# A gated-experts layer on one core: the order of ScalarE's seedings in the first unit, the banks of its fourth slab, and the counts at which turnings and operand steps are issued

## The chip, the core and the metric

The kernel runs on one core of a Trainium2 chip. The metric is the device time of one execution in microseconds. Before the change it is 2478.14 us, the median of three runs (2477.49 to 2479.66). About 0.2% of that, 5 us, is what such a measurement can tell from no change.

## The reference, cut to what matters

There are eight sequences of 512 rows with 256 columns, eight experts and one shared expert, all in float32. Each expert multiplies by a gate matrix and an up matrix (256 x 1024), takes silu(gate) * up, and multiplies by a down matrix (1024 x 256). The experts' outputs are summed with a weight for each sequence and added to the input.

```python
E, B, S, D, F = (8, 2, 256, 256, 1024)   # the input that comes in is (8, 512, 256)
g = jnp.einsum('bsd,edf->ebsf', h, Wg)
u = jnp.einsum('bsd,edf->ebsf', h, Wu)
expert_outs = jnp.einsum('ebsf,efd->ebsd', jax.nn.silu(g) * u, Wd)
expert_output = jnp.einsum('be,ebsd->bsd', gating_probs, expert_outs)
shared = jnp.einsum('bsf,fd->bsd', jax.nn.silu(h @ Sg) * (h @ Su), Sd)
x = x + (1.0 - sg) * expert_output + sg * shared
```

## The kernel before, in words

**Units.** The work is cut into 36 units: two halves `h` of four sequences, nine experts `e` (the ninth is the shared one), two groups `g` of four 128-wide slabs of F. A unit computes silu(gate) * up for four slabs `i` and four sequences `j`, 16 combinations, and then their down products. Everything is held transposed, so a tile is 128 columns of F or D by 512 rows of a sequence.

**Fewer products by sharing.** With the 256 input columns in two halves, each combination would need two matmuls for gate (`m` = 0) and two for up (`m` = 1). The kernel saves some by a bilinear identity over pairs of slabs and sequences. The four "hub" combinations (i, i) take a product P (`P_step`, line 401) and a product Q into the same bank (`Q_step`, line 423). Each of the six pairs in `PAIRS` then takes three products for two combinations: R1 (`R1_step`, line 442), which goes into a bank that was *seeded* with a difference of two P's, and two products R (`R_step`, line 452). With the down products (three for each pair, lines 538, 522 and 561, and eight for the row and column sums, `p` and `q`) a unit has 78 matmuls. Float32 takes two passes, so the trace shows two records for each. In the steady stretch a unit takes 66.95 us (one unit's P at 1378.42, the next unit's at 1445.37), 0.86 us for each matmul.

**Who does what between.** ScalarE copies P to SBUF (line 406), takes silu (line 387, `finish` with m = 0), copies the finished hub bank D (line 429), seeds banks (`seed`, line 437) and copies or scales accumulators. VectorE forms the differences `f` of P's (lines 416 and 418; a slab's differences must be read before Q may go into that bank), multiplies silu by up (line 392, `finish` with m = 1, giving `h`), writes the second bank of a pair as D minus R1 (line 447) and adds D to the other one (line 457). GpSimd (POOL) forms the weights' differences and sums (`w_difference`, line 331; `w_sums`, lines 343 and 344, two of whose operands ScalarE scales at line 341 for three of the six pairs), the down weights' forms (`d_forms`), and the row and column sums of `h` (`add_sum`, line 479). In the first half's first unit it also forms `b` (line 251).

**Banks.** There are eight PSUM banks. Tags `g0` and `g1` have three each for gate and up; `po0` and `po1` are one each and take the down products and all transposes ("turnings"). `new_po` alternates between the last two; while a pair's first down product is `held`, everything else goes to the other one. Two engines' accesses to one bank are put in program order, two reads as well: where `Q_step` calls `finish` and then the copy of D, the copy waits for the multiply.

**The order.** A generator, `gate_up`, yields after each step of gate and up, and `down` after each down product. The strings `FIRST`, `ORDER` and `LAST` interleave them: G is one step of `gate_up`, D one step of `down` of the unit before or of this one. In a unit there are 16 hub steps (`HUB_STEPS`) with 8 D's among them, and then six blocks "GGDGGDGGD", one for each pair. In the first unit ("TGGTGGTGG", then 16 G's, then five blocks) the first D comes only after pair 0's block. `seed(u, 0)` is called ahead of P of slab 3, and `seed(u, p + 1)` at the head of block p. TensorE's and POOL's instructions keep the program's order throughout, ScalarE's in the first unit only; all the rest is ordered by the framework's planner, which works with its own cost estimates.

**The two counters.** `since_close` counts D's. From unit 2 on, at every fourth D one step of `prepare(1)` is taken, which makes the second half's operands: its 72 steps are, for each of four sequences, six (load, nothing, two turnings, nothing, store), and then for each of six pairs, eight (load, nothing, three with POOL subtracts and adds of 128 x 512, two with nothing, store). In the first unit of the second half (unit 18), where the count starts again at 0, the eight finished output blocks of the first half are turned back (`turn_back`, transposes at line 143 into a `po` bank, an add of the input at line 625, a store) at the D's in `BACK_AT`. There D 1 to 11 still belong to the unit before: p0, q0, three of pair 5, q1, p1, q2, p2, q3, p3. After that each pair of unit 18 takes three D's.

Of the kernel before, what the change touches and what calls it, by code (L numbers as in the profile page):

```python
# [9 lines left out]
F32 = mybir.dt.float32  # L10
# [6 lines left out]
def kernel(  # L17
# [37 lines left out]
    nc = tc.nc  # L55
# [322 lines left out]
        u.Ud[p] = U  # L378
        u.Wd[p] = {lo: W[:, 0], hi: W[:, 1]}

    def new_bank(u, m, name):
        return ps_g.tile([P, S], F32, tag=f"g{m}", name=f"{name}{m}_{u.name}")

    def finish(u, m, i, j, bank):
        if m == 0:
            s = spool.tile([P, S], F32, tag="sg", name=f"sg{i}{j}_{u.name}")
            nc.scalar.activation(s, bank, AF.Silu)  # L387
            u.sg[i, j] = s
        else:
            b = NI * u.h + j  # L390
            t = hpool.tile([P, S], F32, tag="h", name=f"h{i}{j}_{u.name}")
            ve.scalar_tensor_tensor(  # L392
                t, u.sg[i, j], coef[:, u.e, b : b + 1], bank, ALU.mult, ALU.mult
            )
            u.h_[i, j] = t


    def P_step(u, i, m):
        bank = new_bank(u, m, f"c{i}{i}")
        u.bank[i, i, m] = bank  # L400
        nc.tensor.matmul(  # L401
            bank, u.raw[i][:, m, 0], xhub[u.h, i][:, 0], start=True, stop=True
        )
        if i < 3:
            t = ppool.tile([P, S], F32, tag="p", name=f"P{i}{m}_{u.name}")
            nc.scalar.copy(t, bank)  # L406
            u.Ps[i, m] = t
        for p, (k, j) in enumerate(PAIRS):
            if max(k, j) == i:

                o = u.Ps[min(k, j), m]
                t = o
                if i < 3:
                    t = zpool.tile([P, S], F32, tag="z", name=f"f{k}{j}{m}_{u.name}")
                if k == i:
                    ve.tensor_sub(t, o, bank)  # L416
                else:
                    ve.tensor_sub(t, bank, o)
                u.f[p, m] = t

    def Q_step(u, i, m):
        bank = u.bank[i, i, m]
        nc.tensor.matmul(  # L423
            bank, u.at[i][:, m], xhub[u.h, i][:, 1],
            start=False, stop=True, skip_group_check=True,
        )
        finish(u, m, i, i, bank)
        t = ddpool.tile([P, S], F32, tag="dd", name=f"D{i}{m}_{u.name}")
        nc.scalar.copy(t, bank)  # L429
        u.Ds[i, m] = t  # L430

    def seed(u, p):

        i, j = PAIRS[p]
        for m in range(2):
            u.bank[j, i, m] = new_bank(u, m, f"c{j}{i}")
            nc.scalar.copy(u.bank[j, i, m], u.f[p, m])  # L437
# [23 lines left out]
    def h_sums(u, p):  # L461


        i, j = PAIRS[p]
        if not starred(u, p):
            return
        u.X[p] = tpool.tile([P, S], F32, tag="t", name=f"X{p}_{u.name}")
        ve.tensor_sub(u.X[p], u.h_[j, i], u.h_[i, j])  # L468
        for k, l in ((i, j), (j, i)):
            for which, n in (("rows", k), ("cols", l)):  # L470
                u.sums.append((which, n, (k, l)))
# [191 lines left out]
    def gate_up(u, nxt):  # L663

        def differences(p):
            x_difference(u, p)
            w_difference(u, p)

        def sums(p):
            x_sums(u, p)  # L670
            w_sums(u, p)

        for p, make in ((0, w_difference), (0, w_sums), (1, w_difference), (1, w_sums)):
            make(u, p)
        if u.n:
            make_at(u, 3)
        w_difference(u, 2)
        ahead = ((0, x_difference), (0, x_sums), (1, x_difference), (1, x_sums), (2, x_difference))
        if u.n:
            for p, make in ahead:  # L680
                make(u, p)
        step = 0
        for kind, i, m in HUB_STEPS:
            if kind == "P" and i == 3 and m == 0:
                seed(u, 0)
            if kind == "Q":
                Q_step(u, i, m)
            elif kind == "P":
                P_step(u, i, m)
                if u.n == 0 and m == 1 and i in (1, 3):  # L690
                    for p, make in ahead[:2] if i == 1 else ahead[2:]:
                        make(u, p)
            else:
                R1_step(u, 0, m)
            step += 1
            if step == 2 and u.n:
                make_ad(u)
            if step in (3, 5, 7, 9, 11, 13) and u.n:
                d_forms(u, (step - 3) // 2)
            yield  # L700
        if u.n == 0:
            make_ad(u)
            for p in range(len(PAIRS)):
                d_forms(u, p)
        for p in range(len(PAIRS)):
            last = p + 1 == len(PAIRS)
            if p + 3 < len(PAIRS):
                differences(p + 3)
            if nxt is not None:
                if p >= 2:  # L710
                    load_w(nxt, p - 2)
                    if p < 5:
                        make_at(nxt, p - 2)
            store_forms(u)
            if p == 5 and nxt is not None:
                load_d(nxt)
            if not last:
                seed(u, p + 1)
            for m in range(2):
                if not last:  # L720
                    R1_step(u, p + 1, m)
                elif nxt is not None:
                    P_step(nxt, 0, m)
                yield
                for r in range(2):
                    R_step(u, p, m, r)
                    if m == 1 and r == 1:
                        h_sums(u, p)
                        if p + 2 < len(PAIRS):
                            sums(p + 2)  # L730
                    yield
# [20 lines left out]

    ends = {}
    since_close = 1000
    BACK_AT = (4, 7, 10, 13, 15, 18, 21, 24)
    HAND = {mybir.EngineType.PE, mybir.EngineType.Pool}
    by_hand = ExitStack()
    by_hand.enter_context(
# [18 lines left out]
    for u in units:  # L777
        final = u.closes
        if u.opens and u.h:
            since_close = 0  # L780
        nxt = units[u.n + 1] if u.n + 1 < len(units) else None
        g = gate_up(u, nxt)
        nG = 0
        for what in FIRST if u.n == 0 else LAST if nxt is None else ORDER:
            if what == "G":
                if nG == TAKE:
                    for _ in behind:
                        pass
                    if u.opens:
                        acc = {}  # L790
                    behind = down(u, acc)
                if final and nxt is not None and nG in (18, 21, 24, 27):
                    load_x(u.h + 1, (nG - 18) // 3)
                if nxt is None and nG == 40:
                    for i in range(NI):
                        last_rows[i] = load_rows(
                            *((zpool, "z") if i < 3 else (iopool, "io")), NI * u.h + i
                        )
                if nG > TAKE and nG % 2 == 0 or nxt is None:
                    for _ in range(2 if nxt is None else 1):  # L800
                        if u.sums:
                            add_sum(u)
                if nG < TAKE and u.n and units[u.n - 1].sums:
                    add_sum(units[u.n - 1])
                next(g)
                nG += 1
            elif what == "T":
                for _ in range(2):
                    next(turning, None)
            elif what == "B":  # L810
                turn_back(u.h, *ENDS.pop(0))
            elif what == "X":
                i, j, pools = TAILS.pop(0)
                if pools:
                    tail_banks(j, pools)
                tail(u, i, j, bool(pools))
            elif what == "S":
                store_rows(STORES.pop(0))
            else:
                next(behind, None)  # L820
                since_close += 1
                if ahead is not None and u.n >= 2 and since_close % 4 == 0:
                    next(ahead, None)
                if u.opens and since_close in BACK_AT:
                    turn_back(u.h - 1, *BACK[BACK_AT.index(since_close)])
        for _ in g:
            pass
        if u.closes:
            for _ in ahead:
                pass  # L830
        if u.n == 0:
            by_hand.close()
            by_hand.enter_context(tc.manual_schedule(engines=HAND))
        for _ in turning:
            pass
# [37 lines left out]
```

## Time and profile before

| what | value |
|---|---|
| median of three runs | 2478.14 us |
| the profiled execution | 2474.26 us, its span 2472.4 us |
| granted TensorE clock, mean | 0.999 |
| PE busy | 2439.9 us, 99% |
| POOL busy | 2100.4 us, 85% |
| DVE busy | 1938.0 us, 78% |
| ACT busy | 1247.4 us, 50% |
| DMA | 103 GB/s mean; the main queue 33.7% of 16 engines' span |
| PE busy in 0 to 40 us / 40 to 80 us | 31.40 us / 36.06 us |
| PE busy in 200 to 1200 us | 995.86 us |
| PE busy in 1240 to 1280 us | 35.55 us |

TensorE is busy nearly all the time, so what can change is the little time in which it waits: at the start, where the two halves meet, at the end, and in single places between. Time at which another engine is idle costs nothing by itself. The last three rows are from the profile's table of stretches (its first rows end at 40, 60 and 80 us).

### The profile page before, as it was taken

The numbers are of one execution on the slowest core, as the hardware profiler recorded it, in microseconds if no ns is written. First come the engines' busy times: TensorE is split into PE (matmuls) and PEld (weight loads), VectorE is DVE, ScalarE is ACT, GpSimd is POOL, SyncE is SP. The second block draws the span as 40 slices with busy tenths as digits, with TensorE's granted clock in tenths as the row PEclk, the third lists the DMA queues.
The fourth block names the chain that finished last, engine by engine and source line by source line (L and its number), as shares of the span: only waits on it lengthen the run. The fifth ranks groups of instructions, "written<-read, shape, count | busy, mean of one in ns | idle before, by whom it ended". The sixth has DMA issues, their size and how long they took to land. (4 is left out here: it accounts for less than half of the span.)

```text
span 2472.4 us, 22803 instructions
## 1 busy us (share of the span) xinstructions
PE 2439.9 (99%) x5772; PEld 1082.1 (44%) x5772; DVE 1938.0 (78%) x2880; ACT 1247.4 (50%) x2305; POOL 2100.4 (85%) x2339
## 2 busy tenths in 40 slices
PE   8999999999999999999999999999999999999998
PEld 3444444444444444444444444444444444444444
DVE  6777777778777787877977777778777777777788
ACT  4554455455545555555445555555555555555552
POOL 7888888998899898888878888888888888888884
PEclk9999999999999999999999999999999999999999
DMA  4333334433333332333443333223333332233332
GB/s 155 93 97 96 111 117 125 132 124 109 112 111 116 99 113 86 102 98 113 126 132 94 94 90 94 85 90 99 102 102 103 94 102 90 85 94 90 94 95 76
DMA packets 180800, 255.81 MB, mean 103 GB/s; under 512 B 14016, under 2 KB 114368, under 8 KB 180672
## 3 DMA queue, kind: packets, MB, share of 16 engines
q1 hardware_dynamic: 180384, 254.33, 33.7%
q8 instruction: 48, 0.79, 0.1%
q14 instruction: 80, 0.66, 0.1%
q10 hardware_dynamic: 288, 0.04, 0.0%
HBM read 238.59 MB, written 15.73 MB: 103 GB/s over the span
## 5 line engine op out<-in xcount | busy, mean ns | idle before, releaser
L452 PE MATMUL c<-b,wb 128*128 128x512 f32 x1728 | 847.3, 592 | 0.8 <-DMA b<-xs 0.8
L387 ACT ACTIVATE sg<-c 128x512 f32<-128x512 f32 x576 | 343.8, 597 | 607.2 <-DVE c L457 346.0
L392 DVE SCALAR_TENSOR_TENSOR h<-sg,coef,c 128x512 f32<-128x512 f32 x576 | 428.1, 743 | 244.4 <-PE c L452 139.6
L452 PEld LDWEIGHTS c<-b,wb 128*128 128x128 f32 x1728 | 327.3, 190 | 409.4 <-issue 385.0
L442 PE MATMUL c<-v,u 128*128 128x512 f32 x864 | 442.5, 594 | 9.7 <-ACT c L437 9.7
L479 POOL TENSOR_TENSOR rows<-rows,h 128x512 f32<-128x512 f32 x284 | 374.7, 1319 | 0.0
L447 DVE TENSOR_TENSOR c<-D,c 128x512 f32<-128x512 f32 x432 | 299.2, 692 | 85.7 <-ACT sg L387 64.2
L479 POOL TENSOR_TENSOR cols<-cols,h 128x512 f32<-128x512 f32 x284 | 362.9, 1278 | 0.0
L457 DVE TENSOR_TENSOR c<-c,D 128x512 f32<-128x512 f32 x432 | 298.8, 692 | 20.1 <-PE c L452 19.9
L343 POOL TENSOR_TENSOR wb<-u,wb 128x256 f32<-128x256 f32 x108 | 80.2, 742 | 240.4 <-ACT wb L341 240.4
L401 PE MATMUL c<-x,w 128*128 128x512 f32 x576 | 276.5, 592 | 0.3 <-DVE x L166 0.3
L442 PEld LDWEIGHTS c<-v,u 128*128 128x128 f32 x864 | 163.2, 190 | 217.3 <-issue 171.1
L538 PE MATMUL r<-h,wd 128*128 128x512 f32 x428 | 218.7, 592 | 1.6 <-DVE accb L513 1.6
L468 DVE TENSOR_TENSOR X<-h,h 128x512 f32<-128x512 f32 x214 | 214.2, 1001 | 7.0
L561 PE MATMUL r<-X,ud 128*128 128x512 f32 x428 | 218.6, 592 | 0.0
L429 ACT COPY D<-c 128x512 f32<-128x512 f32 x288 | 168.3, 584 | 92.1 <-DVE h L392 92.1
L423 PE MATMUL c<-x,at 128*128 128x512 f32 x432 | 210.0, 595 | 0.9 <-DVE P L416 0.9
L479 POOL TENSOR_TENSOR rows<-h,h 128x512 f32<-128x512 f32 x144 | 197.5, 1371 | 0.0
L479 POOL TENSOR_TENSOR cols<-h,h 128x512 f32<-128x512 f32 x144 | 185.7, 1289 | 0.0
L406 ACT COPY P<-c 128x512 f32<-128x512 f32 x216 | 126.6, 587 | 104.7 <-PE c L401 100.4
L401 PEld LDWEIGHTS c<-x,w 128*128 128x128 f32 x576 | 109.1, 190 | 136.4 <-issue 112.4
L521 ACT COPY S<-accS 128x512 f32<-128x512 f32 x135 | 79.7, 590 | 155.4 <-DVE accV L509 145.6
(106 smaller groups left out, 3474.3 us busy)
## 6 DMA issues: line engine op xcount, KB each, us to landing
b<-xs SPq DMA_DIRECT2D x210, 512.0 KB, 3.6
v<-xs SPq DMA_DIRECT2D x210, 256.0 KB, 2.6
w<-in_L_cond_Wg_dram SPq DMA_DIRECT2D x128, 128.0 KB, 3.5
w<-in_L_cond_Wu_dram SPq DMA_DIRECT2D x128, 128.0 KB, 3.6
wd<-in_L_cond_Wd_dram SPq DMA_DIRECT2D x32, 512.0 KB, 4.9
xin<-in_x_dram SPq DMA_DIRECT2D x24, 256.0 KB, 3.7
f<-xd SPq DMA_DIRECT2D x24, 256.0 KB, 3.2
xs<-f SPq DMA_DIRECT2D x18, 256.0 KB, 2.1
```

The source lines that it names most:

```text
L387: nc.scalar.activation(s, bank, AF.Silu)
L392: ve.scalar_tensor_tensor(t, u.sg[i, j], coef[:, u.e, b : b + 1], bank, ALU.mult, ALU.mult)
L401: nc.tensor.matmul(bank, u.raw[i][:, m, 0], xhub[u.h, i][:, 0], start=True, stop=True)
L423: nc.tensor.matmul(bank, u.at[i][:, m], xhub[u.h, i][:, 1], start=False, stop=True, skip_group_check=True,)
L442: nc.tensor.matmul(bank, u.U[p][:, m], u.V[p], start=False, stop=True, skip_group_check=True)
L447: ve.tensor_sub(other, u.Ds[j, m], bank)
L452: nc.tensor.matmul(bank, u.W[p][:, r, m], u.VB[p][:, r], start=False, stop=True, skip_group_check=True,)
L457: ve.tensor_add(bank, bank, u.Ds[j, m])
L468: ve.tensor_sub(u.X[p], u.h_[j, i], u.h_[i, j])
L479: gp.tensor_tensor(sums[n], u.h_[n, n] if first else sums[n], u.h_[at], ALU.add)
L538: nc.tensor.matmul(po, w, b, start=True, stop=True)
L561: nc.tensor.matmul(A, u.Ud[p], u.X[p], start=False, stop=True, skip_group_check=True)
```

## The change

1. In the first unit the two P's of slab 3 go to the `po` banks, not the `g` banks.
2. In the first unit the seeds are issued earlier in ScalarE's order: pair 0's ahead of Q of slab 1, pair 1's ahead of P of slab 3, and pair p + 2's at the end of block p, ahead of the scalings of `w_sums(p + 2)`.
3. In the first unit, for m = 1, the copy of D comes ahead of `finish`, so the multiply on VectorE waits for the copy.
4. The turnings in unit 18 come at other D's.
5. A step of `prepare` comes at every fifth D.

```diff
-    def new_bank(u, m, name):
+    def new_bank(u, m, name, spare=False):
+
+        if spare and u.n == 0:
+            turned[m] = False
+            return ps_o.tile([P, S], F32, tag=f"po{m}", name=f"{name}{m}_{u.name}")
         return ps_g.tile([P, S], F32, tag=f"g{m}", name=f"{name}{m}_{u.name}")
...
-        bank = new_bank(u, m, f"c{i}{i}")
+        bank = new_bank(u, m, f"c{i}{i}", i == 3)
...
+        t = ddpool.tile([P, S], F32, tag="dd", name=f"D{i}{m}_{u.name}")
+        u.Ds[i, m] = t
+        if u.n == 0 and m == 1:
+            nc.scalar.copy(t, bank)
         finish(u, m, i, i, bank)
-        t = ddpool.tile([P, S], F32, tag="dd", name=f"D{i}{m}_{u.name}")
-        nc.scalar.copy(t, bank)
-        u.Ds[i, m] = t
+        if u.n or m == 0:
+            nc.scalar.copy(t, bank)
...
-            if kind == "P" and i == 3 and m == 0:
+            if (kind, i, m) == ("P", 3, 0) and u.n or (kind, i, m) == ("Q", 1, 0) and u.n == 0:
                 seed(u, 0)
+            if (kind, i, m) == ("P", 3, 0) and u.n == 0:
+                seed(u, 1)
...
-            if not last:
+            if not last and u.n:
                 seed(u, p + 1)
...
                         h_sums(u, p)
+                        if u.n == 0 and p + 2 < len(PAIRS):
+                            seed(u, p + 2)
                         if p + 2 < len(PAIRS):
                             sums(p + 2)
...
-    BACK_AT = (4, 7, 10, 13, 15, 18, 21, 24)
+    BACK_AT = (5, 7, 9, 11, 14, 17, 20, 23)
...
-                if ahead is not None and u.n >= 2 and since_close % 4 == 0:
+                if ahead is not None and u.n >= 2 and since_close % 5 == 0:
```

## The prediction

> **What bounds the kernel.** I read the engines' busy times first, then who PE waited for, then the first 80 us engine by engine, then each other place with a wait.
>
> ```profile
> PE 2439.9 (99%) x5772; PEld 1082.1 (44%) x5772; DVE 1938.0 (78%) x2880; ACT 1247.4 (50%) x2305; POOL 2100.4 (85%) x2339
> PE c L442 <- ACT c L437: 9.7, 6, 2.3
> PE q L538 <- POOL cols L479: 2.3, 1, 2.3
> PE pto L143 <- ACT accS L505: 1.9, 1, 1.9
> PE pto L143 <- DVE accB L509: 1.8, 2, 1.4
> PE pto L143 <- DVE accV L511: 1.6, 1, 1.6
> PE ptx L143 <- ACT accS L530: 1.0, 1, 1.0
> PE c L423 <- DVE P L416: 0.9, 2, 0.5
> ```
>
> PE is the bound, and the number of matmuls stays. So the ceiling is the waits, in all about 28 us (the list has some more at the two ends, which the change doesn't touch). The largest is R1 waiting for its seed, 9.7 us in six waits; PE's timeline has all six before 68 us: 2.31, 2.10, 1.35, 1.26, 1.26 and 1.38. The first shows the cause, and a second cost behind it:
>
> ```profile
> 24.61 0.59 ACT L429 COPY D<-c 128x512 f32<-128x512 f32 x1 [1.74 <-DVE h L392]
> 25.10 1.11 ACT L437 COPY c<-f 128x512 f32<-128x512 f32 x2
> 25.84 1.69 PE L442 MATMUL c<-v,u 128*128 128x512 f32 x2 [2.31 <-ACT c L437]
> 26.00:28.00 2.00, 2.00 (x3) 0.60 (x3) 2.00 (x4) 0.21 (x1) 1.92 (x5) 0.55 1.01 381
> 28.00:30.00 2.00, 2.00 (x4) 0.86 (x3) 1.52 (x3) 0.71 (x2) 1.84 (x4) 0.60 0.61 240
> 25.25 3.66 DVE L416 TENSOR_TENSOR P<-P,c 128x512 f32<-128x512 f32 x6
> ```
>
> The seed waits in ScalarE's fixed order behind the copy of D, which waits for VectorE's multiply. After the gap the granted clock (third column from the end in the two stretches) is halved for a while: R00, Q30 and R01 start at 25.84, 27.33, 29.04 and Q31 at 30.19, so 4.35 us for three products that take 2.57 at full clock, 1.8 us lost. The last line matters as much: the six differences that Q30 and Q31 wait for run only from 25.25 to 28.91.
>
> POOL is the second engine. It has no idle from 14.65 on but four waits, and 1.01 at 82.83:
>
> ```profile
> 38.83 1.27 POOL L251 TENSOR_TENSOR b<-v,x 128x512 f32<-128x512 f32 x1 [1.91 <-ACT sg L387]
> 47.26 1.27 POOL L251 TENSOR_TENSOR b<-v,x 128x512 f32<-128x512 f32 x1 [1.74 <-PE c L452]
> 56.48 1.27 POOL L251 TENSOR_TENSOR b<-v,x 128x512 f32<-128x512 f32 x1 [1.29 <-PE c L452]
> 65.70 1.27 POOL L251 TENSOR_TENSOR b<-v,x 128x512 f32<-128x512 f32 x1 [1.32 <-PE c L452]
> 100.28 1.27 POOL L479 TENSOR_TENSOR cols<-cols,h 128x512 f32<-128x512 f32 x1
> 103.12 1.02 PE L538 MATMUL q<-cols,ad 128*128 128x512 f32 x2
> ```
>
> The last pair is q2 of unit 1: its sum ends at 101.55, so POOL is only 1.5 us ahead of PE there.
>
> **The change part by part: the hub of the first unit.** PE ends P31 near 23.4 in both kernels. ScalarE is free at 18.85; pair 0's two copies (0.59 each, 0.49 apart) go from there to 20.0, silu 1 moves from 19.12 to 20.0, and the copies D11 and D21, no longer behind a multiply, end near 21.5 and 23. So no ScalarE work is late, R00 starts at 23.4 and not 25.84, and that 2.31 goes. What is late next is Q30. VectorE has no idle from 15.7 to 29.5, and the change takes no instruction from it; in whichever order the planner puts it (the multiplies now wait for the copies, so fillers will go first), the six differences end near 28.9 as before. So Q30 waits about 3 us from 24.2, Q31 starts at 28.95, and R1 of pair 1, whose seed is long there, at 29.85 and not 33.31: 3.5 us won of 2.31 + 2.10 + 1.8. Bounds: 1.7 us if the clock halves again in the new gap, 6.2 if the planner puts the 3.6 us of fillers (1.04, 1.75, 0.83) behind the differences. I take 3.5, since those fillers run first in the order of before.
>
> The clock row is where a rule and the trace differ. The Trainium skill's "TensorE: Matmul & The Clock Gate", "HAM oscillation", asks for no idle gaps of more than about 3.4 us; by that a gap of 2.3 costs no clock, and the sum would hold 2.31 + 2.10 only, with none of the 1.8 to win. This trace has the halved clock after 2.31 us of idle, and none after 2.10 us at 31.2. The same page ("Part 1") says that the windows run freely, which fits both. I go by the trace: the gap was dear, and the new one of 3 us may be; with the phase of before it falls over two windows (24.2 to 25.8 to 27.2), so I book no loss.
>
> P31 in a `po` bank costs nothing: the last turning's readers end at 17.6 and the first down product comes at 41.86, the bank is read out near 31. The multiply that now waits for the copy (0.59) adds no work: the order of two readers of a bank is turned round, and before the copy waited.
>
> **Blocks 0 to 4.** Block 0 runs from 29.85, six products, to 35.0. Pair 2's first seed follows silu of R001 (product ends 32.4, VectorE's add by 34.4 behind the two scalings' work of 1.6 us, silu to 35.0), so R1 of pair 2 starts at 35.6 against 40.04: 4.45 won. The second seed needs the bank of R011, its multiply ends near 38.5, the seed 39.1, just in time. From there each block drops its wait, 1.26 + 1.26 + 1.38 = 3.9, and I keep 0.35 for seeds that come a little late: 8.0 by PE's own chain. Queued behind the waiting second seed on ScalarE are the two scalings (0.72) and a silu; the scalings come at 39.8 where POOL wants them at 38.2, which makes it idle 1.3.
>
> **POOL's cap.** POOL's idle time until q2 of unit 1 is 1.91 + 1.74 + 1.29 + 1.32 + 1.01 = 7.27. All of it can go, less the 1.3 just named: 6.0. With the 1.5 of lead, PE can be 7.5 us earlier at q2, not 8.0. I take **-7.5** for the first unit; bounds -3.5 (hub alone, 1.7, and half the blocks) and -8.8 (7.27 + 1.5).
>
> **The turnings in unit 18.** Before, PE waits there 1.65 at D4 (the turning goes into the bank that D4 has just written, and two VectorE subtracts read it), 0.41 at D7, 0.47 at Q30 between, and 1.92 at D13 (again the second D of a pair). After, D14, 17, 20 and 23 are third D's, whose free bank was read out one or two products ago, and 9 and 11 have one that is long read. At D5 the turning's bank is free too, but its add (0.69) comes behind the close's three VectorE instructions (0.70 + 1.29), and q1 in that bank waits 0.7, Q30 0.1; D7 keeps 0.5. So 4.45 becomes 1.3: -3.1; bounds -4.4 and 0 (another 0.5 us at each of six turnings). The eight transposes and their DMAs stay the same in number; the first four loads of x land near 870 us, so the shorter spacing of 2 D's doesn't meet a load.
>
> **Steps of `prepare` at every fifth D.** The 72 steps end in unit 15 and not 13, before unit 17 needs them. A POOL step of 1.23 to 1.9 us placed after the last scaled weight of a unit (D20) and ahead of the next unit's D4 stands before q2's sum. Counting D's: before, three such (subtract, scale, two adds) fall before q2 of unit 10, and there PE waits the 2.28 at 713.60. Their time is 4.8 (starts of 679.66, 686.50 and 708.61 and the next ones), so the lead is 2.5. After, unit 12 and unit 15 have a subtract, a scale and one add each, 3.1 to 3.6: 0.6 to 1.1 each. Unit 9 has two adds: nothing. Sum 1.7 against 2.28. A turning right after the second D of a pair waits for a copy, 1.03 at 253.26 (unit 3, D13). After there are two, unit 2 D19 and unit 4 D22: 2.0. Loads on SP's queue move with the steps and can hold b back, as now 0.19 and 0.57: left equal. Together **+0.4**; bounds -2.5 and +3.
>
> **Sum.** -7.5 - 3.1 + 0.4 = -10.2 on the profiled execution's 2474.26: 2464.1. The median of the runs shown is 3.9 above that execution; carried over, 2468.0.
>
> **The rivals.** *The wait moves, not goes* (0.22): the hub's new Q30 gap halves the clock (1.7 left of 3.5), the seeds queue behind VectorE in each block, POOL's cap bites in unit 1, and turnings win half. -3.5 - 1.5 + 0.5 = -4.5: 2473.6. For it speaks VectorE's full row up to 29.5; against it that steady units run the same blocks with no wait. *More goes* (0.10): fillers later, POOL's full 8.8, turnings -4.4: about -13: 2465. *The plan tips* (0.08): VectorE's and ScalarE's order in 35 units is the planner's, and any edit ahead can shift it. The row that shows the price is Q30 waiting 0.47 for the differences, now in units 18 and 35 only; in the other 33 units that is 15.5 us, less the 10.2 won: +5.3, 2483.4. It decides from 0.31 us a unit on. Against it: the pattern repeats every unit with PE never idle. That the change does not do what it says in the first unit is excluded only as far as ScalarE's order there is by hand.
>
> **How the numbers follow.** The forecast has 0.60. About 0.2%, 5 us, is what the measurement can tell from no change. Faster: 0.60 + 0.10 + nearly half of 0.22 = 0.80; within: 0.12; slower: 0.08. Range: 2464 (case three, a little beyond) to 2474 (case two and the poorer ends of two terms); beyond lie the tipped plan and the tails.
>
> **What would show it.** Right: no row "c L442 <- ACT c L437" over 2 us in all, a new wait of 2 to 3 us of L423 on L416 before 30 us, PE reaching unit 1's first Q near 76 and not 83.4, POOL without its four waits, no 1.9 us in unit 18, waits of about 1 us at q2 of units 12 and 15 and after the turnings of units 2 and 4. Wrong: R1 still waiting for seeds, L423 waiting in every unit, or POOL more than 2 us behind at q2 of unit 1.

## The result, and the profile after

The changed kernel takes 2463.04 us, the median of five runs (2462.99 to 2464.21), against 2478.14 (2476.09 to 2479.66): a ratio of 0.9941, 95% interval 0.9927 to 0.9956. That is 15.1 us faster, 10.2 were forecast, and 2463.04 lies just under the range's lower end of 2464.

The profiled execution moved as forecast: 2464.21 us against 2474.26, so 10.05 less where the sum said 10.2. The 5 us that are missing in the forecast lie between profile and timed runs. The execution of after that was profiled is the slowest of its five runs. The one of before was 1.8 us faster than the fastest of its five.

The profile after, first the engines' busy times and then who PE waited for (total, times, longest). Line numbers have moved: R1 is now line 449, Q is 427, `seed` 444, `add_sum` 486.

```profile
PE 2439.2 (99%) x5772; PEld 1082.2 (44%) x5772; DVE 1936.5 (79%) x2880; ACT 1246.9 (51%) x2305; POOL 2100.1 (85%) x2339
PE q L545 <- POOL cols L486: 3.3, 4, 1.2
PE c L427 <- DVE P L420: 2.7, 3, 1.8
PE pto L143 <- DVE accB L516: 1.8, 2, 1.4
PE ptx L143 <- ACT accS L537: 1.8, 2, 0.9
PE c L449 <- ACT c L444: 0.7, 1, 0.7
```

The seeds' row, 9.7 us before, is down to 0.7 in one wait. The two turnings' rows of 1.9 and 1.6 are gone; that of `ptx` has grown from 1.0 to 1.8. Q's wait for VectorE has grown from 0.9 to 2.7, and q's for POOL from one wait to four.

The first unit, from the timelines of PE, VectorE, ScalarE and POOL in turn:

```profile
24.59 1.02 PE L449 MATMUL c<-v,u 128*128 128x512 f32 x2
27.39 1.12 PE L427 MATMUL c<-x,at 128*128 128x512 f32 x2 [1.78 <-DVE P L420]
25.47 3.67 DVE L420 TENSOR_TENSOR P<-P,c 128x512 f32<-128x512 f32 x6
46.85 0.59 ACT L444 COPY c<-f 128x512 f32<-128x512 f32 x1 [4.97 <-DVE h L396]
47.93 0.73 POOL L343 TENSOR_TENSOR wb<-u,wb 128x256 f32<-128x256 f32 x1 [0.64 <-ACT wb L341]
95.11 1.26 POOL L486 TENSOR_TENSOR cols<-cols,h 128x512 f32<-128x512 f32 x1
96.43 1.12 PE L545 MATMUL q<-cols,ad 128*128 128x512 f32 x2 [0.66 <-POOL cols L486]
```

R00 starts with no wait. Q30 then waits 1.78 us for the first half of the six differences, which VectorE runs from 25.47, 0.22 us from where it ran them before. One second seed of a block is issued late (46.85), after ScalarE has waited 4.97 us for VectorE's multiply on its bank, and costs PE 0.72. POOL has one idle of 0.64 left, and q2 of unit 1 waits for it: POOL's lead of 1.5 us is used up.

The clock was halved in this execution as well, but at the start. The line gives the stretch, the engines' busy times and, third from the end, the granted clock:

```profile
8.00:11.00 3.00, 3.00 (x4) 1.04 (x4) 0.00 (x0) 0.59 (x1) 1.25 (x5) 0.51 1.04 318
```

To place the gains, the table compares the start of each unit's first row-sum product, `p0`, between kernels. "Unit 1" is at 85.09 us in the first profile of before; a negative number is earlier.

| profile | unit 1 | unit 2 | unit 17 | unit 19 |
|---|---|---|---|---|
| after | -7.51 | -6.58 | -5.79 | -10.16 |
| after again (`e15_after_again`) | -8.48 | -7.63 | -6.91 | -11.30 |
| before again (`e1_before_again`) | +1.60 | +1.60 | +3.96 | +3.96 |
| before, third profile (`e11_before_look`) | -0.41 | -0.41 | +2.28 | +2.27 |
| before, fourth profile (`e12_before_look2`) | -0.55 | -0.55 | +2.04 | +2.03 |

After unit 19 every row stays as it is to the end.

### The profile page after: what moved, and what is told of

It is laid out like the page before. It is cut to its first block, busy times and chain, and to the rows that moved or that the text cites. A ratio compares the mean times of both kernels' runs of the same rounds, so it can differ in the third digit from the quotient of the medians.

```text
span 2462.3 us, 22810 instructions
## 1 busy us (share of the span) xinstructions
PE 2439.2 (99%) x5772; PEld 1082.2 (44%) x5772; DVE 1936.5 (79%) x2880; ACT 1246.9 (51%) x2305; POOL 2100.1 (85%) x2339
## 4 chain that ended last, share of the span: by engine, by line
PE 89%; POOL 6%; DVE 2%; issue 1%; DMA 1%; ACT 0%; SPq 0%; ACTq 0%; DVEq 0%; POOLq 0%
PE c L459 28%; PE c L449 14%; PE c L427 9%; PE c L405 8%; PE r L545 7%; PE r L568 7%; PE S L529 5%; PE b L529 5%; PE q L545 5%; PE s L545 2%; POOL cols L486 1%; POOL rows L486 1%; POOL wd L376 1%; DVE h L396 1%; POOL wb L343 0%
```

## The experiments

Two theories stood at the start. CLOCK: the waits that the profile shows are the smaller part; behind each long gap TensorE's clock can be halved for 3.41 us, 1.7 us lost, not in every execution, and the change takes these away with the gaps. The rivals: late loads; a fixed offset between profiled and timed runs; or one of the three parts being worth more than its waits.

**The kernel of before again** (no edit).

> The kernel of before once more, unchanged. Its one profiled execution was 2474.26 us, its timed runs 2476.1 to 2479.7: 2 to 5 us more. Theory CLOCK: the idle gaps of the first 34 us halve TensorE's clock for 3.41 us at a time (1.7 us lost each), and how many of them do so differs from execution to execution with the phase of the clock's windows; then the executions spread over 2474 to 2480 in steps of about 1.7 us, and a further profile shows one or more half-clock stretches, at other places than 25.8 us. Rival TRANSFERS: late loads in single places; then the profile shows waits of PE for DMA of some us that the first one lacks. Rival OFFSET: timed runs are always some us above a profiled one; then the profile is again near 2474 with one half-clock stretch.

Measured: 2478.23 us median (2474.16 to 2479.94, 11 runs), its profile 2478.23. It holds two half-clock stretches. One is at 27 us, close to where it was in the first profile; one is new, behind q2 of unit 10, where the wait itself is as long as in the first profile (2.31 against 2.28):

```profile
716.00:720.00 4.00, 3.99 (x6) 1.83 (x7) 0.69 (x1) 0.00 (x0) 3.92 (x5) 0.61 0.30 109
```

The first profile of before has a clock of 1.00 in the same stretch. In the table's terms 1.73 us were lost there (from +2.38 at unit 10 to +4.11 at unit 11), 0.8 in unit 6 at a late load of b, and 1.6 before unit 1, where R00 starts at 27.52 and not 25.84. The start is the clock's as well, it seems: up to 10.3 us the first products take 1.06 us each, as inside after's half-clock stretch, against 0.59 in the first profile. (The record of the clock begins only there in this profile, so the views print 1.00 before it.) So there is no fixed offset. The first profile of before was a lucky one.

**The first unit's parts alone** (`BACK_AT` and `% 4` as before).

> Parts 1 to 3 of the change alone (the first unit's seeds, banks and copies of D); turnings and every-fourth steps as before. By the trace of after PE is 7.5 us earlier at the end of the first unit (unit 1's first Q), less 0.66 of waiting for POOL at q2: profile near 2467, so 7 us under the profile of before. Theory CLOCK: in the timed runs the gain is larger, 10 to 12 us, since the gaps that halved the clock in most executions of before are gone: 2466 to 2468 median. Rival (the rest comes from turnings or steps): 7 us in the timed runs too, 2471.

Measured: 2469.21 us, ratio 0.9962 (0.9949 to 0.9974), 8.8 us under the 2478.04 of before beside it, between the two theories. Its profile has -8.46 at unit 1 and -7.55 at unit 2, with slow first products (1.06 us each up to 10.4 us) and no other half-clock stretch in the first unit. It has two later ones, behind the two gaps that this kernel keeps, 2.28 us at q2 and 1.92 us at the turning after D13:

```profile
708.00:712.00 4.00, 4.00 (x8) 1.65 (x7) 0.70 (x1) 1.40 (x3) 3.76 (x7) 0.73 0.00 0
1266.10 0.75 PE L143 MATMUL pto<-ident,accB 128*128 128x128 f32 x4 [1.92 <-ACT accS L512]
1268.00:1272.00 4.00, 4.00 (x8) 1.63 (x7) 3.06 (x5) 1.48 (x4) 1.18 (x2) 0.76 0.37 100
```

So a gap at a turning can cost the clock as well.

**The turnings alone.**

```diff
-    BACK_AT = (4, 7, 10, 13, 15, 18, 21, 24)
+    BACK_AT = (5, 7, 9, 11, 14, 17, 20, 23)
```

> The other BACK_AT alone. The traces show 4.45 us of waits at the second half's opening before and 0.90 after: -3.5 us, 2474.6. It leaves the first unit as it is, so theory CLOCK gives the same 3.5 in the timed runs and a spread as wide as that of before; the rival that the unexplained 4.9 us comes from the turnings gives -8.

Measured: 2470.53 us, ratio 0.9971 (0.9960 to 0.9981), 7.5 us under before, nearer to the rival. Its profile places 4.4 us in unit 18 (+0.48 at unit 17, -3.89 at unit 19), not 3.5. The other 3 us of the timed runs it doesn't place. The seven runs spread from 2469.60 to 2475.82; by means instead of medians the gain is 6.0.

**PE's first gaps filled.** Sixteen transposes of a constant ahead of R00, and likewise ahead of pair 1's first R1:

```diff
+    FILL = 4
...
+                if u.n == 0 and m == 0:
+                    for k in range(FILL):
+                        pt, n = new_po(f"fill{k}")
+                        turned[n] = True
+                        turn(pt, [ident] * NT)
                 R1_step(u, 0, m)
```

> The kernel of before with sixteen transposes of a constant (1.76 us) put on PE just ahead of the first unit's R00 and again just ahead of pair 1's first R1, where PE waits 2.31 and 2.10 us for a seed. They add work that nothing reads and take away nothing but idle time. Theory CLOCK: the clock no longer halves there, so the timed runs are 2 to 5 us faster than before (2473 to 2476) and the spread shrinks. Rivals (TRANSFERS, OFFSET): no gain, the median stays within 1 us of before or rises by up to 0.5 us.

Measured: 2476.98 us against 2478.04, ratio 0.9994 (0.9985 to 1.0002): 1.1 us, less than forecast, and the interval holds no change. The profile has no half-clock stretch before 100 us and has the one behind q2. The fill isn't free, though: R00 starts at 26.77, 0.9 later than in the first profile of before, and at unit 1 this profile stands at +0.15, although that first one had lost 1.7 us to the clock by then. The slowest of 11 runs is at 2477.5, where the kernel of before beside it had runs up to 2482.2, one of 2869.85 left aside.

**Every fifth D alone** (`% 5` for `% 4`).

> Every fifth D alone. The waits that go with the steps (q2 of one unit 2.28, a turning 1.03, loads about 0.8) become three of 0.5 to 1.2 at q2, two of 0.9 after turnings, 0.2 for loads: +0.5 us by the waits. Theory CLOCK: the gap of 2.28 us at q2 of unit 10 halved the clock after it in three of the five profiles with steps at every fourth D (1.7 us each), and none of the new gaps is over 1.2; so 1 us is won there: median 0.5 us under before, 2477.5. Rival (waits are all): 0.5 us over before.

Measured: 2477.86 us, ratio 1.0009 (0.9997 to 1.0021): no difference that can be told. Its profile can't be used for the sum: the clock was granted at 0.95 for its first 490 us, in an execution of 2494.7. Its waits at q2 (three, at most 1.2) and of turnings for a copy (two, at most 0.8) are those counted.

**The first unit and the turnings** (the whole change with `% 4`).

> The whole change but steps at every fourth D as before. Waits alone: 0.5 us faster than the whole change, 2462.5. Theory CLOCK: the 2.28 us gap at q2 of unit 10 is back and halves the clock in about three of five executions, so the executions fall into two groups 1.7 us apart, near 2462 and 2464, where those of the whole change lie within 1.2 us.

Measured: 2463.92 us (2462.25, 2462.38, 2463.92, 2464.19, 2464.66), ratio 0.9948 (0.9936 to 0.9959). The runs do fall into two groups about 2 us apart. But the profile, of 2464.19, has no half-clock stretch behind its 2.27 us gap at q2, and one of the slower three ran at a mean clock of 1.000, so the groups' cause is not shown. What the profile has is a wait of 2.23 for a block's second seed, where after has 0.72.

**The turnings, with the three other gaps filled** (the fill above, and twelve transposes ahead of q2 of unit 10).

> The other BACK_AT alone, and PE's three other long gaps filled with transposes of a constant that nothing reads (sixteen ahead of R00, sixteen ahead of pair 1's first R1, twelve ahead of q2 of unit 10). No gap of over 1.5 us is left between 12 us and the last unit, and all waits for seeds are still there. Theory CLOCK: the executions lie together near their value without a half-clock stretch, 2469 to 2471, none at 2474 to 2476 as with the other BACK_AT alone. Rival: spread and median as there, 2470.5 with runs up to 2476.

Measured: 2470.19 us (2468.90 to 2470.59, 8 runs), ratio 0.9973 (0.9964 to 0.9983). The median is that of the turnings alone; the runs at 2474 and 2476 are gone, and the profile has no half-clock stretch until the end. All eight ran at a mean clock of 1.000; the two slow runs of the turnings alone had 0.997, the other five 0.999. The spread speaks for CLOCK, the median for neither.

**Another phase of the steps** (the whole change with `since_close % 4 == 2`).

> The whole change, but the steps of the operands at D's whose count leaves 2 when divided by 4, not at multiples of 5. Counted D by D: no unit then has more than 2.5 us of POOL steps ahead of q2 (its lead), and one turning comes right after the second D of a pair. Waits that go with the steps: 1.0 against 4.6 in the whole change, so 3 to 3.5 us faster, 2459.5 to 2460.5; no gap over 1.8 us left to halve the clock. Rival (POOL's lead is less than 2.5 when two adds stand ahead, or loads hold b back): 1 us faster or none.

Measured: 2462.76 us, ratio 0.9946 (0.9933 to 0.9959), so no gain of 3 us. The rival held: q2's waits fell from 3.3 to 1.4, and waits for loads of b, of which after has none, came to 3.1:

```profile
PE c L459 <- DMA b<-xs: 3.1, 3, 1.2
PE q L545 <- POOL cols L486: 1.4, 3, 0.6
```

**The hub part without the block part.**

```diff
-            if not last and u.n:
+            if not last and (u.n or p >= 1):
                 seed(u, p + 1)
...
-                        if u.n == 0 and p + 2 < len(PAIRS):
-                            seed(u, p + 2)
```

> The whole change, but from pair 2 on the seeds are issued at the head of the block again, behind the scalings (pair 0's and pair 1's stay early, slab 3's P in the po banks, D ahead of the multiply). Theory: the hub part and the block part are separate terms; the waits of the blocks (1.35, 1.26, 1.26, 1.38 before) come back, less the 0.72 and the 0.66 at q2 that the change still waits: 3.9 to 4.6 us slower than the whole change, 2467 to 2467.7, PE at unit 1's first row-sum product near 81.5 to 82. Rival (POOL or VectorE set the pace of the blocks, so early seeds win little there): under 2 us slower, 2465.

Measured: 2466.74 us, ratio 0.9956 (0.9940 to 0.9973), 3.7 us over the 2463.04 of after, which ran on another chip: a little less than the 3.9 to 4.6 forecast. All four block waits are back:

```profile
PE c L449 <- ACT c L444: 5.1, 4, 1.3
```

At unit 1 it stands at -5.57 with no half-clock stretch, where the four profiles with the block part and a start at full clock have -8.14 to -8.81. So the early seeds of the blocks win 2.6 to 3.2 us at unit 1. At unit 2 the lead over it is 1.6 to 2.4, since without them q2 of unit 1 doesn't wait for POOL.

**The copy of D behind the multiply again.**

```diff
-        if u.n == 0 and m == 1:
-            nc.scalar.copy(t, bank)
         finish(u, m, i, i, bank)
-        if u.n or m == 0:
-            nc.scalar.copy(t, bank)
+        nc.scalar.copy(t, bank)
```

> The whole change without its part 3: for m = 1 the copy of D comes behind the multiply again in the first unit. Theory (VectorE's row of work sets Q30): ScalarE waits for the multiplies again, silu 2 and the seeds of pair 1 slip by 1 to 2 us, but those seeds have 4 us to spare; Q30's wait moves by no more than 0.7, the total stays within 1 us of the whole change. Rival (the copies' order is what frees ScalarE): R1 of pair 1 waits 2 us for its seed again and the run is 2 us or more slower.

Measured: 2464.30 us, ratio 0.9945 (0.9930 to 0.9960). Its profile is like that of after all the way: unit 1 at -7.28 (-7.51), Q30 waits 1.78 (1.78), a half-clock stretch at the start in both. Part 3 is worth nothing that can be seen.

**Two more profiles of before** (no edit).

> The kernel of before unchanged, one more profiled execution: a look at what differs between executions of the same kernel. Theory CLOCK: the time above 2472.5 us is 1.7 us for each half-clock stretch of 3.41 us, with a few tenths to 1 us at the start and where PE waits for a load; the stretches begin at the ends of gaps of 1.9 us or more. Rival: two profiles differ by more than 1 us in a place where neither clock nor a load differs.

Measured: 2476.50 us. Half-clock stretches at 32.5 us, behind the second gap of the first unit, and behind q2. 0.8 us were lost at a load in unit 6.

> As the run before it, once more: the same kernel, the same two theories.

Measured: 2476.27 us. Half-clock stretches at 8.0 us and behind q2, and a wait of 1.31 for a load in unit 11:

```profile
712.00:716.00 4.00, 2.80 (x5) 1.35 (x6) 0.69 (x1) 1.00 (x2) 3.92 (x5) 0.82 0.46 142
716.00:720.00 4.00, 4.00 (x8) 1.63 (x7) 1.21 (x2) 1.77 (x3) 3.76 (x7) 0.76 0.00 0
```

R00 starts at 24.84 in one and 26.80 in the other, which had its half-clock stretch at the start. From unit 1 on, all differences of more than 0.3 us between the four profiles of before are a half-clock stretch or a load of b.

**Another remainder of five** (`since_close % 5 == 2`).

> The whole change, but the steps come at D's whose count leaves 2 when divided by 5. Counted D by D: at most 2.5 us of POOL steps ahead of any unit's q2, and two turnings right after a second D. Theory (POOL's place decides): of the 4.6 us of waits that go with the steps, the 2.66 at q2 of units 10 to 16 fall to 0.5 at most, the turnings' 1.9 stay: 2 us faster than the whole change on the same chip. Rival (loads, as with remainder 2 of 4, where three waits of 3.1 us for b took the gain back): no faster.

Measured: 2464.03 us, against 2462.99 for the whole change beside it: no gain. The waits at q2 fell as counted (0.47, 0.41, 0.26, 0.27 and unit 1's 0.62), but the turnings' rose to 2.4. At unit 17 the profile is 0.1 us ahead of after's second one, and it was 0.3 ahead at unit 1. The counting places the waits; what one place saves another takes.

**Before, with three gaps filled** (both fills, turnings as before).

> The kernel of before with its three long gaps at a wait for a seed (two) and at q2 of unit 10 filled with transposes of a constant that nothing reads. All waits stay. Theory CLOCK: the stretches behind these gaps, seen in all four profiles of before (two in each of three, one in the other, one of them at the start of the run instead), are gone: profile without a half-clock stretch between 12 us and the end, median 2.5 to 3.5 us under before, 2474 to 2475. Rival (the profiles' stretches are not what the timed runs lose): within 1 us of before.

Measured: 2474.90 us against 2476.13 beside it, ratio 0.9993 (0.9984 to 1.0002). The profile has slow first products up to 9.6 us and no half-clock stretch from there to the end. The waits for seeds and turnings are all there, and q2's is down to 0.43 behind the fill. Eleven runs lie within 2472.99 to 2475.83, those of before beside it within 2473.39 to 2480.98. The size of the median's move, 1.2, misses the forecast of 2.5 to 3.5, and the interval holds no change. What the runs with fills lack is the slow end.

**The changed kernel again** (no edit).

> The changed kernel once more, unchanged. It has one gap of 1.78 us near 27 us and none over 1.2 until the last unit. Theory CLOCK: the executions lie within 2 us of each other (2462.5 to 2464.5), 14 to 15.5 us under the median of before on the same chip, and the profile has at most one half-clock stretch, at the start. Rival: a spread as wide as that of before, 5 us.

Measured: 2462.99 us (2462.66 to 2463.63), ratio 0.9944 (0.9931 to 0.9956). That is 13.1 us under the 2476.13 of before beside it, less than the 14 to 15.5 forecast. The spread is 1.0 us as forecast, that of before beside it 7.6. The profile, 2463.05, has no half-clock stretch until the end: at the stretch that cost the first profile of after 1.7 us it lost nothing.

## Why the prediction was wrong, point by point

**The step that failed** is the last one of the sum: "The median of the runs shown is 3.9 above that execution; carried over, 2468.0". It took the distance between one profile and the timed runs for something that both kernels have. It belongs to before alone: the median of before lies 3.9 above its profile, that of after 1.2 under its own. The four profiles of before are 2474.26, 2478.23, 2476.50 and 2476.27. The first has one half-clock stretch; the others have two each, slow first products besides in the second, and 0.7 to 0.8 us more at a load. The two profiles of after are 2464.21 and 2463.05, with one and none. Mean against mean that is 12.7 us, between the 10.05 of the first pair and the 15.1 of the runs. The working had the halved clock in its hand: 1.8 us were counted behind one gap of 2.31 us. It did not ask what the same clock does behind the gaps of 2.28 and 1.92 in other executions. Behind q2's gap it was halved in three of four profiles of before, 1.7 us each.

The timed runs tell the same, since each has its mean granted clock on record (not those of before beside the first five of after). Of 77 executions of before on four chips (that of 2869.85 left aside), 35 at 0.999 took 2476.0 us on average, 26 at 0.998 took 2477.7, and 14 at 0.997 took 2480.0; two at 1.000 took 2474.3. A thousandth of the clock is 2.5 us of the span. The ten of after lie at 0.999 and 1.000. From these means, which are given to three digits, an estimate: before loses 4.1 us an execution to the clock and after 0.7, where the first pair of profiles lost 1.7 and 2.0. So some 3.7 of the missing 5 us are the clock's. In the changed kernels the clock no longer orders the runs: with the steps at remainder 2 of 4 the two at 1.000 took 2464.5 and 2465.2, the three at 0.999 at most 2462.8.

**The rule and the row.** The limit of about 3.4 us for an idle gap in the Trainium skill's "TensorE: Matmul & The Clock Gate", "HAM oscillation", is not what these profiles show: the clock was halved behind gaps of 1.92, 2.06 to 2.10 and 2.28 to 2.84, and not behind others of the same length. What decides is how much of a gap falls into one window of the clock. In every profile but that of every fifth D alone, the changes of clock lie whole multiples of 3.413 us apart, and so mark the windows out. That the windows run freely, as the same page's "Part 1" has it, agrees with this: they begin 0.1 to 2.9 us into the span, differently from profile to profile. Here is q2's gap in the first profile of before, where two windows share it, and then in that of before again, where it lies in one (window; PE's busy time first, the clock third from the end):

```profile
708.87:712.28 3.41, 2.45 (x6) 0.76 (x4) 2.80 (x5) 2.52 (x6) 3.33 (x5) 1.00 0.41 134
712.28:715.69 3.41, 2.10 (x5) 1.06 (x6) 0.69 (x1) 1.13 (x2) 3.33 (x5) 1.00 0.54 172
715.69:719.11 3.42, 3.42 (x9) 1.52 (x8) 1.40 (x2) 1.96 (x4) 3.26 (x6) 1.00 0.00 2
713.44:716.85 3.41, 1.10 (x3) 0.49 (x3) 0.95 (x2) 1.47 (x3) 3.33 (x5) 1.00 0.75 229
716.85:720.27 3.42, 3.42 (x5) 1.35 (x4) 0.69 (x1) 0.00 (x0) 3.26 (x6) 0.50 0.12 46
```

The table has the other windows that bear on it:

| profile and gap | window | PE idle in it | clock in the next |
|---|---|---|---|
| before, R00 | 22.78 to 26.20 | 2.31 | 0.50 |
| before, third profile, pair 1's R1 | 29.11 to 32.52 | 2.09 | 0.50 |
| before, fourth profile, q2 of unit 10 | 711.12 to 714.53 | 2.08 | 0.50 |
| turnings alone, R00 | 23.43 to 26.84 | 2.06 | 0.50 |
| turnings alone, pair 1's R1 | 30.25 to 33.66 | 1.97 | 1.00 |
| before again, D13's turning | 1273.23 to 1276.64 | 1.92 | 1.00 |
| first unit alone, D13's turning | 1263.11 to 1266.52 | 1.92 | 0.50 |
| after, Q30 | 24.60 to 28.01 | 1.78 | 1.00 |

Between 12 and 2400 us of these 16 profiles, all nine windows with 2.06 us of idle time or more were followed by one at half clock, one of five at 1.92 to 1.97 was, and none below. So the length of q2's gap stayed at 2.3 and its cost was 0 or 1.7, by where the windows lay. The prediction booked no loss for the new gap at Q30 because it would fall over two windows; it took the boundary at 25.8, where its own rows have the clock halved from 26.2. No loss came, but for another reason: in both profiles of after the gap lies in one window and is short, 1.78 and 1.23 us. That much was luck.

**The hub** held in kind. The seed's wait went, and Q30 waits for VectorE, 1.78 us in the first profile of after where about 3 were forecast. R1 of pair 1 starts at 30.15 (29.85 forecast), though the start of that execution lost 1.7 us to the clock. Part 3 costs nothing, as forecast, and brings nothing. The tipped plan did not come: after the first unit Q30 waits in units 18 and 35 only (0.49 and 0.47), as before.

**The blocks and POOL's cap** held. At q2 of unit 1 POOL's lead is gone and PE waits 0.66; at unit 2 the two profiles of after are 6.6 and 7.6 us earlier, where -7.5 was forecast. The seed said to be "just in time" came 0.72 late, in a later block, and up to 2.23 late in other profiles.

**The turnings** were mis-sized: -3.1 forecast, -4.4 measured (from unit 17 to unit 19 in the table, in both profiles of after). D9 to D23 have no wait left, as forecast. Q1's wait of 0.7 after D5 did not come. The rest is that a wait costs more than its idle row: unit 18 took 76.23 us from p0 to p0 before and 71.86 after, where 78 matmuls and eight turnings of 0.43 make 70.4. So 5.8 us of excess stand against 4.45 us of listed waits, and 1.5 against 0.90. The lines of before at Q30 show where it goes:

```profile
1250.26 1.02 PE L442 MATMUL c<-v,u 128*128 128x512 f32 x2
1251.76 1.13 PE L423 MATMUL c<-x,at 128*128 128x512 f32 x2 [0.47 <-DVE P L416]
1252.72 1.02 PE L522 MATMUL b<-rows,wd 128*128 128x512 f32 x2
```

A product's line lasts 1.02, but the next one can start 0.86 after it, so the idle row counts 0.16 too little; and the product behind the wait has its successor 0.96 after it. That makes 0.2 to 0.3 us more for each wait. Another 0.4 of the 5.8 is a slip near 1297 us that no row lists.

**The steps** were near: +0.4 forecast, +0.7 to +0.8 from unit 2 to unit 17. Their waits fell at the units counted: q2 of units 12 and 15 (0.96 and 1.19, 0.6 to 1.1 forecast), unit 9 (0.51, none forecast), and turnings of units 2 and 4 (0.95 and 0.80).

**What stays open.** The turnings alone gained 7.5 us in timed runs by medians and 6.0 by means, 1.6 to 3 more than any profile places. Runs of before above 2478.3 were seen in no profile; their mean clocks are on record, but not the places where it was halved. The fills' medians moved by about 1 us, less than the stretches in the profiles would give; in the profile of the first two gaps filled the later R00 took it back. Part 1, the banks of slab 3, was in no run taken away alone.

## What to carry to other kernels

Where PE is the bound, a profile shows what its waits cost in that one execution; before a sum is carried to a median, look at a second profile of the same kernel and ask what each gap does at its worst. Here a gap was worth its length, 0.2 to 0.3 us more, and 1.7 us on top in those executions in which more than 2 us of it fell into one window of the clock; a gap of 1.8 us was short enough to be safe once the first products were past. When waits are taken from one engine's order, the next limit can be read ahead from the other engines' rows: VectorE's unbroken row gave Q30, POOL's lead at one product gave the cap.

## What the runs showed of the hardware that was not expected

The clock was halved for one window of 3.413 us when PE had been idle for 2.06 us or more in the window before, and in one case of five for 1.92 to 1.97: far less than a whole window. Since the windows lay differently against the span in each execution, one and the same gap of 2.3 us halved the clock in some executions and not in others. With short matmuls and waits at the start less was enough: in after the window from 4.12 to 7.54 us, with 1.73 us of idle time, was followed by one at half clock, as were windows with 1.62 in two other profiles. In four profiles the first products ran at the half-clock length of 1.06 us until 9.6 to 10.4 us, where the record of the clock begins. Once, in the profile of every fifth D alone, the granted clock was 0.95 for 490 us, for no cause that the profile shows.
